# Cross-attention in fp32: a quarter of the score weights by a fast block algorithm, with three engines' work put in a new order

## The chip, the cores and the metric

The kernel runs on one NeuronCore of a Trainium2 chip. The core has a matrix engine (TensorE, PE in the profile; its weight loads are PEld), a vector engine (VectorE, DVE), an activation engine (ScalarE, ACT), a general engine (GpSimd, POOL) and a queue for transfers (SyncE, SP). The metric is device time in microseconds (us) of one execution. Everything is fp32.

## What is computed

```python
Q, K, V = x @ Wq, c @ Wk, c @ Wv        # 16 batches: x 256x256, c 77x192; 8 heads of 256
score = Q K^T / sqrt(256)                # per batch and head 256x77, masked
attn  = softmax(score)
out   = concat_heads(attn V) @ Wo + x
y     = (out - mean(out)) * rsqrt(var(out) + 1e-5) * gamma + beta
```

## The kernel before, in words

The kernel never forms Q, K or V. At the start it forms per head G = Wk Wq^T/16 (192 x 256; rows 0 to 127 in `gA`, the last 64 rows of two heads side by side in `gB`) and U = Wv Wo (in `uA`, `uB`). The context lies transposed, rows 0 to 127 in `cA` and the other 64 in both halves of `cB`. Then, for a group of GB = 4 batches and for each head, A = G^T c (256 x 308, as two halves `dc` of 128 rows), and scores are x A. For a batch, VW = c U.

A tile is 128 rows of x; a batch b has two tiles, 2b and 2b+1. The order of work is written out by hand: the program runs each engine's instructions as the code names them, and a wait on another engine blocks everything behind it on its own engine. The loop over batches `for b in range(-1, B - 1)` does in one step: scores of batch b+1 on TensorE (`scores`, L303), masking and row maximum on VectorE (`shift`, L320), exponentials on ScalarE (`exponential`, L340), weights on GpSimd (`weigh`, L361: exponentials times 1/sum into `p`), their transposition on VectorE (`turn`, L371), the sums of blocks that the next product needs on GpSimd (`sums`, L431 to L434; `differences`, L414), and for batch b the product of weights and VW by seven block products (`seven`, L450), whose results VectorE adds to x from PSUM (`add_product`, L498) and GpSimd from a copy `m` (`add_seven`, L484). For batch b-1 it takes the statistics of the rows (`finish`, L506 and L509 on VectorE), the inverse deviation (`spread`, L527 and L528 on ScalarE) and the normalisation (`normalise`, L548 and L577 on VectorE).

Every second step also prepares two batches ahead: `prepare_vw` (pv, L227 and L238) twice, and twice a pair of heads of A for the next group: `prepare_a` (pa), in part A with 128 rows of contraction (L193, four tiles of 128x32 of the array at a time) and in part B with 64 rows (L205, eight tiles of 64x32). ScalarE copies both out of PSUM (L963). PSUM is one pool of eight banks; a bank comes free when its last reader is through, and the next tile of the program takes the bank that has been free longest.

Of the kernel before, what the change touches and what calls it, by code (L numbers as in the profile page):

```python
# [27 lines left out]
def kernel(  # L28
# [53 lines left out]

    def by_dc(ap):
        return ap.rearrange("p (dc i c) -> p i dc c", dc=2, c=BK)
# [15 lines left out]
    cRA = const.tile([P, B, KR], F32, tag="cRA", name="cRA")  # L100
    cRB = const.tile([P, B, KR], F32, tag="cRB", name="cRB")
# [12 lines left out]

    def flat(ap):
        return ap.rearrange("p a b -> p (a b)")
# [51 lines left out]
    def prepare_a(g, places, lo=0, hi=GB, rest_first=False):  # L168
# [16 lines left out]
        def cols(dc, i):  # L185
            return slice((2 * i + dc) * BK, (2 * i + dc + 1) * BK)
# [29 lines left out]
        return part_A, part_B, copies  # L216

# [94 lines left out]
    def shift(t):  # L312


        b, ps = t // QT, ps_of.pop(t)
        s = sp.tile([P, H, S2], F32, tag="s", name=f"s_{t}")
        top = st.tile([P, H], F32, tag="top", name=f"top_{t}")
        for h in range(H):
            a, k = divmod(h, H // 2)
            nc.vector.tensor_tensor_reduce(  # L320
                s[:, h],
                ps[a][:, k * S2 : (k + 1) * S2],
                bias[:, b, :],
                scale=-1.0,
                scalar=FAR,
                op0=ALU.add,
                op1=ALU.min,
                accum_out=top[:, h : h + 1],
            )
        s_of[t] = s, top  # L330

# [105 lines left out]
    def seven(b):  # L437
# [36 lines left out]
        m = vwp.tile([P, 4, P], F32, tag="m", name=f"m_{b}", bufs=1)  # L474
# [3 lines left out]
    def add_seven(b):  # L478

        m = m_of.pop(b)  # L480
        y = x_of(QT * b, QT).rearrange("p t (c d) -> p t c d", c=2)

        def add(to, what):
            nc.gpsimd.tensor_tensor(to, to, what, ALU.add)  # L484

        for i in range(QT):
            add_product(QT * b + i)
# [12 lines left out]
    def finish(t):  # L500
        if t in po_of:
            add_product(t)
        g, j = t // GT, t % GT
        y = x_of(t)[:, 0, :]
        bn = st.tile([P, 6], F32, tag="bn", name=f"bn_{t}")
        nc.vector.bn_stats(bn, y)  # L506
        if j == 0:
            mv_of[g] = st.tile([P, GT, 2], F32, tag="mv", name=f"mv_{g}", bufs=2)
        nc.vector.bn_aggr(mv_of[g][:, j, :], bn)  # L509
# [12 lines left out]
    def spread(first, last):  # L522
# [4 lines left out]
        nc.scalar.activation(log[:, lo:hi], mv_of[g][:, lo:hi, 1], AF.Ln, bias=eps)  # L527
# [72 lines left out]
    with tc.tile_pool(name="wonce", bufs=1) as wp:  # L600
# [204 lines left out]
        def g_of(e):  # L805
# [6 lines left out]
            nc.scalar.mul(gA[:, e], pg, D ** -0.5)  # L812
# [15 lines left out]
        def g_of_pair(a):  # L828
# [12 lines left out]
            for e, o in enumerate(banks):  # L841
                nc.scalar.mul(gA[:, 2 * a + e], o, D ** -0.5)
# [42 lines left out]
        for a in range(1, NF):  # L885
# [7 lines left out]
            a_of_pairs(a, rest_first=True)  # L893
        load_x(0)
# [10 lines left out]
        for j in range(NF // 2):  # L905
# [13 lines left out]
            for e, pw in enumerate(  # L919
# [3 lines left out]
                for i in range(2):  # L923
                    for k in range(2):
                        copy(
                            of_e(uB, e)[half(k), :, 2 * j + i],
                            pw[half(i)].rearrange("p (n c) -> p n c", c=BK),
                        )
        for t in range(QT):
# [4 lines left out]
        turn_rest_last()  # L934
        sum_of(uB)
        for t in range(QT):
            exponential(t)
            weigh(t)

# [10 lines left out]
    def work_of(b, rest_first=False):  # L950
        g, n = b // GB + 1, b % GB
        work = [prepare_vw(b, rest_first)]
        if g < NG - 1 or g == NG - 1 and n < NF // 2:
            work.append(prepare_a(g, (n,), rest_first=rest_first))
        elif b <= NS:
# [11 lines left out]
    def turn_x_and_normalise(g, n, old):  # L967
        to_turn = (g, 0) if g < NG and n == 2 else (g - 1, GT // 2) if g > 1 and n == 0 else None
        if to_turn:
            for j in range(to_turn[1], to_turn[1] + GT // 2, 2):  # L970
                transpose_x(to_turn[0] * GT + j)
        if old:
# [4 lines left out]
    for b in range(-1, B - 1):  # L977
# [3 lines left out]
        for t in new if b >= 0 else ():  # L981
            scores(t)
        for t in new if b >= 0 else ():
            shift(t)
            if b == B - 2:
                finish(t - 2 * QT)
# [5 lines left out]
        for m in range(0, 2) if b < 0 else range(b + 2, min(b + 3, B // 2)):  # L992
            turn_last(m)
        alone = b + 1 >= B - GB // 2
        works = work_of(b + 1) if alone or n % 2 == 0 else []
        for part_A, _, _ in works:
# [21 lines left out]
        for i, t in enumerate(new if b >= 0 else ()):  # L1018
            exponential(t)
            if old:  # L1020
                finish(old[i])
            weigh(t)
        ahead = works and not alone
        if old and not ahead:
            spread(old[0], old[-1] + 1)
        if ahead:
            copy_out(works)
            if old:
                spread(old[0], old[-1] + 1)
# [3 lines left out]
            for part_A, _, _ in works:  # L1033
# [6 lines left out]
        if b < NS:  # L1040
            if now:
                seven(b)
            if old:
                invert(old[0], old[-1] + 1)
                normalise(old[0])
            for t in new:
                turn(t)
            if b < 0:
                for t in range(QT, GT, 2):
                    transpose_x(t)  # L1050
                bias_of(GB, B)
# [8 lines left out]
            if now:  # L1060
                add_seven(b)
# [56 lines left out]
```

## Time and profile before

| what | us |
|---|---|
| time before, median of 3 runs (270.31 to 270.97) | 270.63 |
| the profiled execution's own time | 269.95 |
| its span in the profile | 268.2 |
| busy: TensorE, VectorE, GpSimd, ScalarE | 262.5, 185.9, 173.2, 157.6 |

The profile has one row per group of instructions: line, engine, operation, what it writes and reads, shapes, count, total and mean time, and the idle time of the engine ahead of it with what ended that. The chain of waits follows the execution back from its last instruction and lists in order of time what each stretch of the span went to. Each fp32 matmul of the program is two instructions in the trace: sixteen matmuls of `prepare_a` stand there as x32.

### The profile page before, as it was taken

What the parts mean: (1) busy time and instruction counts of PE and PEld (TensorE: products, weight loads), DVE (VectorE), ACT (ScalarE), POOL (GpSimd) and SP (SyncE); (2) the same over time, 40 slices, a digit from 0 to 9 for tenths busy, and PEclk for the clock granted to TensorE, in tenths of its full rate; (3) what the DMA queues carried; (4) which work ended last, traced back from release to release, by engine and by line L of the source; (5) the groups of instructions that cost most, each with busy time, mean ns of one, the idle gap of its engine ahead of it and who ended that gap; (6) DMA issues with size and microseconds to landing.
All of it is one profiled execution on the core that took longest, in us unless ns stands there. A gap on an engine that the chain in (4) does not pass through costs nothing.

```text
span 268.2 us, 14455 instructions
## 1 busy us (share of the span) xinstructions
PE 262.5 (98%) x6090; PEld 191.8 (72%) x6090; DVE 185.9 (69%) x808; ACT 157.6 (59%) x667; POOL 173.2 (65%) x240
## 2 busy tenths in 40 slices
PE   8999999999999999999999999999999999999992
PEld 8566578944984699459944995499669957985662
DVE  1555967493583868665886379647977887799785
ACT  3243336536857565955596468737775595636772
POOL 1042005728399739994799669965998799585452
PEclk9999999999999999999999999999999999999999
DMA  6989987901500130232012401340034010100112
GB/s 190 217 199 228 334 138 142 311 21 34 129 7 2 46 80 2 63 111 71 5 43 90 112 5 43 91 113 2 6 120 122 4 45 2 44 22 22 46 40 80
DMA packets 41696, 22.69 MB, mean 85 GB/s; under 512 B 24144, under 2 KB 40608, under 8 KB 41632
## 3 DMA queue, kind: packets, MB, share of 16 engines
q1 hardware_dynamic: 41248, 20.98, 30.1%
q0 software_dynamic: 384, 0.79, 1.3%
q8 instruction: 48, 0.79, 1.3%
q14 instruction: 16, 0.13, 0.2%
HBM read 17.57 MB, written 4.19 MB: 81 GB/s over the span
## 4 chain that ended last, share of the span: by engine, by line
PE 98%; DVE 1%; issue 0%; DVEq 0%
PE ps L303 25%; PE pa L193 13%; PE pv L227 11%; PE po L450 11%; PE pm L450 8%; PE pa L205 6%; PE pv L238 6%; PE po L383 4%; PE pu L773 3%; PE pr L263 2%; PE pgb L834 2%; PE pw L787 1%; PE idle L703 1%; PE pr L274 1%; PE phb L850 1%; PE po L399 1%
## 5 line engine op out<-in xcount | busy, mean ns | idle before, releaser
L340 ACT ACTIVATE s<-s,top 128x77 f32<-128x77 f32 x256 | 85.3, 346 | 44.2 <-DVE top L320 37.9
L303 PE MATMUL ps<-a,xT 128*32 128x154 f32 x2048 | 69.9, 294 | 0.0
L303 PEld LDWEIGHTS ps<-a,xT 128*32 128x32 f32 x2048 | 66.2, 110 | 1.2 <-issue 0.4
L361 POOL TENSOR_TENSOR p<-s,rden 128x512 f32<-128x512 f32 x64 | 47.5, 768 | 29.5 <-DVE rden L355 29.4
L320 DVE CUSTOM_DVE_ANT_0 s<-ps,bias 128x77 f32<-128x77 f32 x256 | 43.5, 232 | 14.3 <-PE ps L303 14.3
L340 ACT ACTIVATION_READ_ACCUMULATOR s<-s,top 128x1 f32 x224 | 42.0, 187 | 0.0
L193 PE MATMUL pa<-cA,gA 128*32 128x308 f32 (+1 forms) x576 | 36.6, 395 | 0.0
L193 PEld LDWEIGHTS pa<-cA,gA 128*32 128x32 f32 x576 | 18.3, 110 | 21.0 <-issue 7.0
L484 POOL TENSOR_TENSOR xg<-xg,m 128x256 f32<-128x256 f32 x39 | 28.7, 736 | 6.6 <-DVE xg L498 4.5
L577 DVE SCALAR_TENSOR_TENSOR xg<-xg,rstd,bet 128x256 f32<-128x256 f32 x27 | 22.9, 847 | 14.0 <-ACT rstd L528 12.6
L227 PE MATMUL pv<-uA,cA 128*32 128x512 f32 x256 | 30.6, 595 | 0.0
L371 DVE STREAM_TRANSPOSE pT<-p 128x640 f32<-128x640 f32 x32 | 25.5, 821 | 3.4 <-POOL p L361 3.3
L414 POOL TENSOR_TENSOR ts<-vw 128x768 f32<-128x768 f32 x13 | 24.0, 1848 | 5.9 <-ACT vw L963 5.9
L963 ACT COPY vw<-pv 128x512 f32<-128x512 f32 x32 | 17.8, 584 | 14.8 <-PE pv L227 8.3
L498 DVE TENSOR_TENSOR xg<-po,xg 128x256 f32<-128x256 f32 x31 | 11.5, 405 | 13.8 <-PE po L450 13.3
L320 DVE DVE_READ_ACCUMULATOR2_ANT top<- 128x1 f32 x256 | 20.8, 81 | 0.0
L205 PE MATMUL pa<-cB,gB 64*32 64x308 f32 (+2 forms) x512 | 20.4, 387 | 0.0
L963 ACT COPY a<-pa 128x308 f32<-128x308 f32 (+1 forms) x56 | 18.9, 395 | 1.9 <-PE pa L193 0.4
L205 PEld LDWEIGHTS pa<-cB,gB 64*32 64x32 f32 (+1 forms) x512 | 11.0, 110 | 11.4 <-issue 6.2
L548 DVE SCALAR_TENSOR_TENSOR xg<-xg,mv,gam 128x256 f32<-128x256 f32 x30 | 17.6, 588 | 0.1
L238 PE MATMUL pv<-uB,cB 64*32 64x512 f32 x256 | 17.3, 597 | 0.0
L227 PEld LDWEIGHTS pv<-uA,cA 128*32 128x32 f32 x256 | 7.5, 109 | 12.8 <-issue 9.9
(119 smaller groups left out, 404.1 us busy)
## 6 DMA issues: line engine op xcount, KB each, us to landing
xg<-in_x_dram SPq DMA_DIRECT2D x8, 512.0 KB, 4.4
xT<-in_x_dram SPq DMA_DIRECT2D x56, 64.0 KB, 2.6
out_dram<-xg SPq DMA_DIRECT2D x11, 256.0 KB, 2.2
wo<-in_L_xattn_Wo_dram SPq DMA_DIRECT2D x4, 512.0 KB, 7.8
wq_blk<-in_L_xattn_Wq_dram SPq DMA_DIRECT2D x12, 128.0 KB, 4.3
out_dram<-xg SPq DMA_DIRECT2D x10, 128.0 KB, 1.9
wk_blk<-in_L_xattn_Wk_dram SPq DMA_DIRECT2D x12, 96.0 KB, 3.6
wvT<-in_L_xattn_Wv_dram POOLq DMA_DIRECT2D x8, 96.0 KB, 6.6
```

The costliest lines, as they stand in the source:

```text
L193: nc.tensor.matmul(flat(o[i * BK : (i + 1) * BK]), gA[:, h, cols(dc, i)], flat(cA[:, batches, :]), start=not rest_first and n in opening, ...
L205: nc.tensor.matmul(flat(banks[j + k][i * BK : (i + wide) * BK]), gB[half(k), h // 2, dc * P + i * BK : dc * P + (i + wide) * BK], flat(cB[ ...
L227: nc.tensor.matmul(pv[k][i * BK : (i + 1) * BK], cA[:, b, k * BK : (k + 1) * BK], uA[:, parts, :, i], start=not rest_first, stop=rest_first,)
L238: nc.tensor.matmul(pv[k][i * BK : (i + 1) * BK], cB[half(k), b, k * BK : (k + 1) * BK], uB[half(k), parts, :, i], start=rest_first, stop=n ...
L303: nc.tensor.matmul(ps[m // 2][i * BK : (i + 1) * BK, m % 2 * 2 * S2 : (m % 2 + 1) * 2 * S2], xT_of[t // PT][:, j * NM + m, dc], flat(a_of[ ...
L320: nc.vector.tensor_tensor_reduce(s[:, h], ps[a][:, k * S2 : (k + 1) * S2], bias[:, b, :], scale=-1.0, scalar=FAR, op0=ALU.add, op1=ALU.min ...
L340: nc.scalar.activation(s[:, h], s[:, h], AF.Exp, bias=top[:, one], scale=-1.0, accum_out=den[:, one] if summed_by_act(t) else None,)
L361: nc.gpsimd.tensor_tensor(part, e_mh[:, :, :, keys], rden_mh.unsqueeze(3).to_broadcast(list(part.shape)), ALU.mult,)
L371: nc.vector.transpose(pT_of[t].rearrange("p n m q -> p m n q"), p.rearrange("p m (n k) -> p m n k", k=BK),)
L450: nc.tensor.matmul(out[i * BK : (i + 1) * BK], weight[:, i], moving, start=first and n == 0, stop=final and n == len(terms) - 1,)
L484: nc.gpsimd.tensor_tensor(to, to, what, ALU.add)
L963: nc.scalar.copy(dst, src)
```

## The change

For 10 of the 12 pairs of heads in groups 1 to 3, A is computed by `prepare_fast` instead of `prepare_a`. With the 4 batches split into two of 154 columns and the 256 rows of A into two blocks of 128, the upper 128 rows of the contraction are a product of 2x2 blocks, done in seven block products; the 64 rows in `gB` take four more: 11 where 12 stood. Each has 64 rows of contraction and 128 rows of result, and runs as two 64x64 tiles of the array with 154 columns; two heads are walked together, one in each half of the rows. One block product per head is copied out of PSUM by ScalarE, and four additions per head on VectorE (`put_together`) make A out of the rest. The sums of blocks of G (`gS`, `gC`) are formed once, and those of c (`cT`, `cD`) at the start and once for each of groups 2 and 3, all on GpSimd with copies on ScalarE.

The loop up to batch 9 is rewritten as pairs of steps, `long_step` and `short_step`. In the long step all part As of `prepare_vw` come first, then `seven`, then part Bs, then the two fast pairs of heads. On GpSimd the weights of new tiles stand ahead of the additions of the previous batches (`add_blocks`), on VectorE the additions to x stand between the two turns, and the statistics of the first 14 tiles are taken by two ScalarE instructions each. From batch 9 on the loop is as before.

```diff
+    def sums_of_g():
+        for parts, sums, e, own, other in parts_of_g():
+            nc.scalar.copy(sums[own, 0, e], parts[other, 1, e])
+            nc.scalar.copy(gC[own], gB[other, :, P:])
+        for parts, sums, e, own, other in parts_of_g():
+            s1, s2, s3 = (sums[own, n, e] for n in range(3))
+            add(s1, s1, parts[own, 1, e])
+            subtract(s2, s1, parts[own, 0, e])
+            subtract(s3, parts[own, 0, e], parts[own, 1, e])
...
+    def sums_of_c(lo, hi):
+        xs, ys = halves_of(cA, lo, hi)
+        t1, t2, t3, t4 = (cT[:, n, lo - 1 : hi - 1] for n in range(4))
+        subtract(t1, ys, xs)
+        for own, other in ((low, high), (high, low)):
+            nc.gpsimd.tensor_copy(t2[own], ys[other])
+        subtract(t3, t2, ys)
+        subtract(t2, t2, t1)
+        for own, other in ((low, high), (high, low)):
+            nc.gpsimd.tensor_copy(t4[own], t2[other])
+        subtract(t4, xs, t4)
...
+    def prepare_fast(g, u):
...
+                for i in range(2):
+                    for ((bank, n), weight, moving), (start, stop, _) in zip(pair, flags):
+                        nc.tensor.matmul(
+                            bank[half(i), n],
+                            weight(i),
+                            moving,
+                            start=start,
+                            stop=stop,
+                        )
+                for ((bank, n), _, _), (_, _, one) in zip(pair, flags):
+                    if one:
+                        nc.scalar.copy(blocks[lone[id(bank)]][:, 0], by_batch(bank)[:, n])
...
+        def put_together(e):
+            mid, end, of = by_batch(mids[e]), by_batch(ends[e]), blocks[e]
+            plus(of[:, 3], mid[:, 2], of[:, 0])
+            plus(of[:, 1:3], mid[:, 0:2], of[:, 3:4].to_broadcast([P, 2, HB, S2]))
+            plus(of[:, 3], mid[:, 0], of[:, 2])
+            plus(of[:, 0:3], end, of[:, 0:3])
...
+        if by_act(t):
+            mean, var = (mv_of[g][:, j, n : n + 1] for n in range(2))
+            nc.scalar.activation(junk, y, AF.Identity, scale=1.0 / DI, accum_out=mean)
+            nc.scalar.activation(junk, y, AF.Square, bias=mean, scale=-1.0, accum_out=var)
+            return
...
         def turn_rest():
             nc.vector.transpose(flat(cA)[:, rest], flat(cA)[:, rest])
-            nc.gpsimd.tensor_copy(cRA, cA[:, :, KM:])
+            nc.scalar.copy(cRA, cA[:, :, KM:])
...
+    def long_step(b):
+        now, new, old = tiles_of(b), tiles_of(b + 1), tiles_of(b - 2)
+        g, n = (b + 1) // GB + 1, (b + 1) % GB
+        statistics(old)
+        if now:
+            scores_and_masks(new)
+            for t in new:
+                exponential(t)
+        while behind:
+            behind.pop(0)()
...
+        works = work_of(b + 1) + work_of(b + 2)
+        for part_A, *_ in works:
+            part_A()
+        if now:
+            seven(b)
+        for _, part_B, _ in works:
+            part_B()
+        fasts = []
+        for k in range(2):
+            fasts.append(prepare_fast(g, n + k))
+            if k == 0:
+                copy_out(works[:1])
+            fasts[k][0]()
+            if k == 0:
+                copy_out(works[1:])
...
+            for i, t in enumerate(new):
+                weigh(t)
+                for t in old[i : i + 1]:
+                    normalise(t)
+            add_blocks(b - 1)
+            turn(new[0])
+            add_products(b)
+            turn(new[1])
+            sums(b + 1)
+            add_blocks(b)
+            for k in range(2):
+                differences(b + 1 + k)
+            if n == 2 and g < NG - 1:
+                sums_of_c(g + 1, g + 2)
+        statistics(tiles_of(b - 1))
+        turn_some_x(g, n)
...
+        fasts[0][1](0)
+        fasts[0][1](1)
+        fasts[1][1](0)
+        behind.append(partial(fasts[1][1], 1))
```

The three pieces below show the order at the places that the steps of the sum speak of. TensorE, the preparation for batches 4 and 5, which lies between the scores of tiles 8 and 9 and those of tiles 10 and 11 (pv is VW, pa is A, pf is A by the fast way). Before, its head:

```order
L227 MATMUL pv_4_0_1850<-uA_79,cA_81 32x512 x4
L227 MATMUL pv_4_1_1851<-uA_79,cA_81 32x512 x4
L193 MATMUL pa_2_0_0_0_1853<-cA_81,gA_77 32x308 x4
L193 MATMUL pa_2_1_0_0_1854<-cA_81,gA_77 32x308 x4
L193 MATMUL pa_2_0_1_0_1855<-cA_81,gA_77 32x308 x4
L193 MATMUL pa_2_1_1_0_1856<-cA_81,gA_77 32x308 x4
L238 MATMUL pv_4_0_1850<-uB_80,cB_82 32x512
```

After, from the last products of `seven` for batch 3 (po) over the end of part B into the first fast pair of heads:

```order
L622 MATMUL po_3_1980<-ts_3_1594,pT_7_1916 32x128 x8
L404 MATMUL pv_4_0_1958<-uB_83,cB_85 32x512
...
L404 MATMUL pv_5_1_1962<-uB_83,cB_85 32x512
L361 MATMUL pf_2_0_0_2065<-cA_84,gA_77 64x154
L361 MATMUL pf_2_0_0_2064<-cA_84,gA_77 64x154
...
L361 MATMUL pf_2_0_0_2065<-cA_84,gS_518 64x154
L361 MATMUL pf_2_1_1_2067<-cA_84,gA_77 64x154
...
L361 MATMUL pf_2_1_1_2066<-cA_84,gA_77 64x154
```

The 308-column products in strips of 32 are gone, the 64x64 products of 154 columns stand at the end, and `seven` moved in between parts A and B.

VectorE, in the same stretch. Before, around the turns of tiles 8 and 9 (p is GpSimd's weights, po the product that is added to x):

```order
L509 BN_AGGR mv_0_1346<-bn_5_1930 128x2
L355 RECIPROCAL rden_9_1933<-den_9_1921 128x8
L548 SCALAR_TENSOR_TENSOR xg_1_518<-xg_1_518,mv_0_1346,gam_69 128x256
L577 SCALAR_TENSOR_TENSOR xg_1_518<-xg_1_518,rstd_4_1944,bet_90 128x256
L371 STREAM_TRANSPOSE pT_8_2086<-p_0_85 128x4x5x32
L371 STREAM_TRANSPOSE pT_9_2088<-p_1_86 128x4x5x32
L165 STREAM_TRANSPOSE xT_3_1441<-xT_3_1441 128x512 x2
...
L498 TENSOR_TENSOR xg_1_518<-po_3_2017,xg_1_518 128x256 x2
```

After, around the same turns in the long step:

```order
L527 RECIPROCAL rden_9_2174<-den_9_1944 128x8
L731 SCALAR_TENSOR_TENSOR xg_0_529<-xg_0_529,mv_0_1604,gam_69 128x256
L760 SCALAR_TENSOR_TENSOR xg_0_529<-xg_0_529,rstd_2_1835,bet_92 128x256
L543 STREAM_TRANSPOSE pT_8_2186<-p_0_87 128x4x5x32
L676 TENSOR_TENSOR xg_1_531<-po_3_1980,xg_1_531 128x256 x2
L543 STREAM_TRANSPOSE pT_9_2190<-p_1_88 128x4x5x32
L175 STREAM_TRANSPOSE xT_3_1617<-xT_3_1617 128x512 x2
L373 TENSOR_TENSOR a_2_2063<-pf_2_0_0_2064,a_2_2063 128x2x77
L373 TENSOR_TENSOR a_2_2063<-pf_2_0_0_2064,a_2_2063 128x4x77
```

The additions to x moved between the two turns, and the additions that make A stand behind them.

GpSimd at the start of the program, from its last loads to the sums of U (`uA`); nan and bias are the mask. Before:

```order
L618 DMA wvT_3_146<-in_L0_xattn_Wv_dram 32x6x128 x2
L594 TENSOR_TENSOR nan_0_621<-nan_0_621 128x4
L595 TENSOR_TENSOR nan_0_621<-nan_0_621 128x4
L596 TENSOR_TENSOR bias_89<-bias_89,nan_0_621 128x308
L902 TENSOR_TENSOR uA_79<-uA_79 128x512
L903 TENSOR_TENSOR uA_79<-uA_79 128x512
```

After:

```order
L801 DMA wvT_3_148<-in_L0_xattn_Wv_dram 32x6x128 x2
L245 TENSOR_TENSOR gS_518<-gS_518,gA_77 64x4x128
L246 TENSOR_TENSOR gS_518<-gS_518,gA_77 64x4x128
L247 TENSOR_TENSOR gS_518<-gA_77 64x4x128
...
L777 TENSOR_TENSOR nan_0_634<-nan_0_634 128x4
L778 TENSOR_TENSOR nan_0_634<-nan_0_634 128x4
L779 TENSOR_TENSOR bias_91<-bias_91,nan_0_634 128x308
L1087 TENSOR_TENSOR uA_82<-uA_82 128x512
L1088 TENSOR_TENSOR uA_82<-uA_82 128x512
L255 TENSOR_TENSOR gS_518<-gA_77,gS_518 64x4x128 x2
```

Six operations on blocks of G now stand ahead of the mask, and two more behind the sums of U.

More of the change, by code (lines that the diff above doesn't have):

```diff
@@ L526, in spread @@
         rstd = st.tile([P, GT], F32, tag="rstd", name=f"rstd_{first}")
-        nc.scalar.activation(log[:, lo:hi], mv_of[g][:, lo:hi, 1], AF.Ln, bias=eps)
+        nc.scalar.activation(log[:, lo:hi], mv_of[g][:, lo:hi, 1], AF.Ln, bias=eps, scale=1.0 / DI if by_act(first) else 1.0)
         nc.scalar.activation(rstd[:, lo:hi], log[:, lo:hi], AF.Exp, scale=-0.5)
@@ L976, with tiles_of, statistics, scores_and_masks @@
     last = NT - 1
-    for b in range(-1, B - 1):
+    def tiles_of(b):
+        return range(b * QT, (b + 1) * QT) if b >= 0 else ()
+    def statistics(tiles):
+        for t in tiles:
+            finish(t)
+        if tiles:
+            spread(tiles[0], tiles[-1] + 1)
+            invert(tiles[0], tiles[-1] + 1)
+    between = []
+    def scores_and_masks(new, to_finish=()):
+        for t in new:
+            scores(t)
+        for i, t in enumerate(new):
+            shift(t)
+            for t in to_finish[i : i + 1]:
+                finish(t)
+            while between:
+                between.pop(0)()
@@ new lines, in short_step, with last_turn @@
+    def short_step(b):
+        new = tiles_of(b + 1)
+        scores_and_masks(new)
+        for t in new:
+            exponential(t)
+        seven(b)
+        weigh(new[0])
+        for _ in range(2):
+            if behind:
+                behind.pop(0)()
+        for m in range(b + 2, min(b + 3, B // 2)):
+            turn_last(m)
+        weigh(new[1])
+        turn(new[0])
+        def last_turn():
+            turn(new[1])
+            sums(b + 1)
+            add_products(b)
+            if b + 1 == ready:
+                add_blocks(b)
+        between.append(last_turn)
@@ L978 @@
+    ready = B - GB - GB // 2 - 1
+    for b in range(-1, ready, 2):
+        long_step(b)
+        short_step(b + 1)
+    statistics(tiles_of(ready - 2))
+    behind.extend(partial(normalise, t) for t in tiles_of(ready - 2))
+    for b in range(ready, B - 1):
         old = range(max(b - 1, 0) * QT, b * QT)
@@ L980 @@
         new = range((b + 1) * QT, (b + 2) * QT)
[L981 to L986, printed above, removed]
+        scores_and_masks(new, old if b == B - 2 else ())
         while behind:
@@ L991 @@
             load_x((g * GB + n) // 2)
-        for m in range(0, 2) if b < 0 else range(b + 2, min(b + 3, B // 2)):
-            turn_last(m)
         alone = b + 1 >= B - GB // 2
-        works = work_of(b + 1) if alone or n % 2 == 0 else []
-        for part_A, _, _ in works:
+        ahead = not alone and n % 2 == 0
+        works = work_of(b + 1) if alone or ahead else []
+        for part_A, *_ in works:
             part_A()
@@ L1040 @@
         if b < NS:
[L1041 to L1045, printed above, removed]
+            seven(b)
+            invert(old[0], old[-1] + 1)
+            normalise(old[0])
             for t in new:
                 turn(t)
[L1048 to L1051, printed above, removed]
             if alone or ahead:
```

176 lines of the change are left out of this document (149 added, 27 removed).

## The prediction

> **What bounds the kernel now.** I read the page's busy line and its chain first, then the chain in order of time, then the groups.
>
> ```profile
> PE 262.5 (98%) x6090; PEld 191.8 (72%) x6090; DVE 185.9 (69%) x808; ACT 157.6 (59%) x667; POOL 173.2 (65%) x240
> PE 98%; DVE 1%; issue 0%; DVEq 0%
> ```
>
> TensorE is busy for 98% of the span, and 98% of the chain lies on it. The chain in time order (start, length) shows that it never pauses:
>
> ```profile
> 17.16 2.21 PE pa L193 x32
> 19.37 1.03 PE phb L850 x32
> 20.41 1.73 PE pgb L834 x32
> ...
> 130.76 4.19 PE ps L303 x128
> 134.95 1.72 PE pv L227 x16
> 136.67 2.07 PE pa L193 x32
> 138.74 1.02 PE pv L238 x16
> 139.76 1.04 PE pa L205 x32
> 140.79 0.86 PE pv L238 x16
> 141.65 1.04 PE pa L205 x32
> 142.69 1.85 PE pv L227 x16
> 144.54 2.07 PE pa L193 x32
> 146.62 1.75 PE pm L450 x64
> 148.37 2.17 PE po L450 x64
> 150.54 4.19 PE ps L303 x128
> ...
> 263.37 0.30 DVE xg L516
> ```
>
> Each stretch starts where the last one ended; the tail off TensorE begins at 263.37. So the change gains only what it takes from TensorE's own work, and loses whatever wait it opens there.
>
> **TensorE's own work.** Two pairs of heads of A take 2 × (2.07 + 1.04) = 6.22 us in each pair of steps (136.67 and 139.76, 141.65 and 144.54). They become 2 × 44 matmuls of 64x64 tiles with 154 columns, 88 trace instructions for each pair of heads. No row shows this shape. The nearest by columns is ps: 4.19/128 = 32.7 ns each at 154 columns, four tiles at a time. The nearest by tile are pgb and phb (64x64): 1.73/32 = 54 ns at 256 columns, 1.03/32 = 32.2 ns at 128. At 256 columns a 64x64 tile costs 0.211 ns a column, ps 0.212: the same pace. At 128 it costs more than that pace (27 ns), because loading weights fills the time:
>
> ```profile
> 19.37:20.41 1.04, 1.04 (x37) 1.01 (x40) 0.00 (x0) 0.42 (x1) 1.04 (x3) 1.00 0.88 208
> ```
>
> (TensorE busy 1.04, weight loads busy 1.01 of 1.04 us.) At 154 columns the columns themselves need 32.6 ns by that pace, as much as the loads took there, so I take ps's 32.7: 88 × 32.7 = 2.88 us. As upper bound, the straight line between phb and pgb gives 32.2 + 26/128 × 21.8 = 36.6 ns, 3.22 us; phb's 1.03 also holds the change of tile shape behind pa, so this is generous. Lower bound: 154 × 0.211 = 32.5 ns, 2.86 us.
>
> Changing the shape of the tiles costs something: pv in part A takes 1.72 behind ps (both 128x32) but 1.85 behind part B, and part B 1.02 against 0.86. Before, each pair of steps has two such changes. After, there are three: part A and `seven` (both 128x32) to part B (64x32), part B to the fast products (64x64), these to the scores (128x32). The middle one keeps 64 rows and changes only the columns; no row shows that alone. I take 0.13, the smaller of the two seen; bounds 0 and 0.16.
>
> Here a rule bears. The Trainium skill (TensorEngine Tiling (Array Packing), Key Properties) says that changing the tiling mode, unlike moving to another tile of the same mode, drains TensorE. By that rule the middle change costs like the others (gain 1.7 us in all), without it nothing (2.3 us); the rows 1.85 and 1.02 agree with a drain where the number of rows changes, and no run here shows the other kind.
>
> Sum for a pair of steps: 6.22 − 2 × 2.88 − 0.13 = 0.33 us; five pairs: 1.65 us. Bounds: 6.22 − 5.72 = 0.50 (2.5 in all), and 6.22 − 6.44 − 0.16 = −0.38 (1.9 slower in all). `seven` and pv keep their shapes, so their move costs TensorE nothing.
>
> **The other engines' work** in a pair of steps, from the busy row of one (VectorE, ScalarE, GpSimd: third to fifth) and the groups:
>
> ```profile
> 130.76:158.64 27.88, 27.88 (x713) 20.22 (x708) 18.59 (x96) 18.15 (x82) 22.53 (x30) 1.00 0.21 60
> L498 DVE TENSOR_TENSOR xg<-po,xg 128x256 f32<-128x256 f32 x31 | 11.5, 405 | 13.8 <-PE po L450 13.3 <-PE po L383 0.5
> L516 DVE TENSOR_TENSOR xg<-po,xg 128x128 f32<-128x128 f32 x2 | 0.6, 286 | 0.0
> L506 DVE BATCH_NORM_STATS2 bn<-xg 128x6 f32<-128x256 f32 x31 | 12.3, 396 | 0.1
> L509 DVE BATCH_NORM_AGGREGATE mv<-bn 128x2 f32<-128x6 f32 x31 | 5.6, 182 | 1.1
> L963 ACT COPY a<-pa 128x308 f32<-128x308 f32 x40 | 15.3, 437 | 1.5
> L963 ACT COPY a<-pa 128x154 f32<-128x154 f32 x16 | 3.5, 292 | 0.4 <-PE pa L193 0.4
> L561 ACT ACTIVATE xg<-xg,rstd 128x256 f32<-128x256 f32 x3 | 1.5, 510 | 0.3 <-DVE xg L548 0.2
> L340 ACT ACTIVATION_READ_ACCUMULATOR s<-s,top 128x1 f32 x224 | 42.0, 187 | 0.0
> L903 POOL TENSOR_TENSOR uA<-uA 128x512 f32<-128x512 f32 x1 | 1.3, 1275 | 0.1
> L484 POOL TENSOR_TENSOR m<-m 128x128 f32<-128x128 f32 x26 | 11.9, 457 | 3.1 <-ACT m L475 2.1
> ```
>
> - VectorE: by the two additions (286 ns at 128 elements, 405 at 256; 0.93 ns an element) a head's four additions of 154, 308, 154 and 462 cost 0.31 + 0.45 + 0.31 + 0.60 = 1.67 us, four heads 6.7. Statistics of four tiles leave: 4 × 0.578 = 2.3. 18.6 + 6.7 − 2.3 = 23.0 of 27.6.
> - ScalarE: eight copies of 308 leave (3.5), four of 154 come (1.2), and eight statistics passes (510 + 187 ns each, 5.6): 18.2 − 3.5 + 1.2 + 5.6 = 21.5.
> - GpSimd: 22.5, and in two pairs of steps the sums of c: four of 154 (0.55 each by L484) and four copies (under that), at most 4.4: 26.9.
>
> All fit under 27.6, so none becomes the bound by its load; the question is lateness. Moved loads of x land two pairs of steps ahead of their use and are priced at nothing; what hides them is that distance.
>
> **Where TensorE could wait.** Time runs from the start of a long step's scores (0). Scores end at 4.19, part A at 7.6, `seven` at 11.55, part B at 13.4; the fast products run from 13.6 to 19.3. The first pair of heads needs four banks: two that `shift` frees (by 4.9), one freed by ScalarE's copy m, and one, at its third block products (14.1), freed by the second addition to x, which now stands on VectorE behind the turn of the first new tile.
>
> ```profile
> 124.11 0.36 ACT L340 ACTIVATE s<-s,top 128x77 f32<-128x77 f32 x1 [2.92 <-DVE top L320]
> ...
> 129.60 0.28 ACT L527 ACTIVATE log<-mv,eps 128x2 f32<-128x2 f32 x1
> 128.95 3.16 POOL L361 TENSOR_TENSOR p<-s,rden 128x512 f32<-128x512 f32 x4 [3.36 <-DVE rden L355]
> ```
>
> Two tiles' exponentials take 5.5 us there (124.11 to 129.60). With ScalarE's statistics ahead of them (2.8 us and 0.5 for the deviation, begun when the short step's copy m is out) they run from about 3.6 to 9.1; VectorE then normalises (1.4), turns the first tile by 11.4 and adds to x by 12.4, after `seven` at 11.55. Margin 1.7 us. GpSimd's weights for a tile (1.6) are ready before. The next scores, at 19.3, need the first head's banks: the first pair of heads ends at 16.4, its first head is put together by 18.1, the second by 19.8 (needed 21.4). Margins 1.2 and 1.6. The mask of the next tile starts some 0.8 us late, which ScalarE's idle 2.92 covers. I price waits at nothing; what is late next if this fails is the mids bank at 14.1.
>
> **The start of the program.** GpSimd gets six sums of G (1.28 each by L903: 7.7 us) ahead of the mask:
>
> ```profile
> 40.16 0.20 POOL L594 TENSOR_TENSOR nan<-nan 128x4 f32<-128x4 f32 x1 [18.46 <-DVE nan L593]
> 40.72 0.70 POOL L596 TENSOR_TENSOR bias<-bias,nan 128x308 f32<-128x308 f32 x1
> 44.91 0.24 DVE L320 CUSTOM_DVE_ANT_0 s<-ps,bias 128x77 f32<-128x77 f32 x1
> ```
>
> It idled 18.46 us there. The sums start when ScalarE has copied A's last banks and the first block, near 32.5, and end near 40.2: just in front of the mask. The mask is ready at 41.4 and wanted at 44.91, so 3.5 us are left.
>
> **Sum.** The profiled execution took 269.95, 0.68 below the median: 269.95 − 1.65 = 268.3 on its scale, 270.63 − 1.65 = 269.0 on the median's.
>
> **Rivals.**
> 1. *Short columns cost more.* The straight line's 36.6 ns would make the pair 0.35 longer than before: 270.63 + 1.75 = 272.4; halfway (34.7 ns) it saves nothing: 270.6. For it: phb. Against it: its loads, not its columns, set that time, and ps shows nothing extra at 154. The Trainium skill (TensorEngine Tiling (Array Packing), Instruction Overhead) speaks for it, with about 60 cycles for each matmul. The trace's ps row does not bear it out: 154 columns at 32.7 ns are half of pa's 64.7 at 308. Chance 0.14.
> 2. *Lateness on VectorE and ScalarE eats the gain.* If the additions for A run 40% slower beside GpSimd (2.35 us a head), three heads end at 23.5 instead of 21.5, the next mask starts 2.0 us later than priced, ScalarE with it, and the margin of 1.7 at 14.1 is gone: TensorE waits 0.3 us a pair, which cancels the gain. For it: VectorE's load grows most, and GpSimd is busy 22.5 of 27.9 beside it. Against it: the additions' rows above are means beside a busy GpSimd already. Time 270 to 271. Chance 0.15.
> 3. *Slower: the mask at the start.* If a sum on 64 partitions takes 2.5 us instead of 1.28, the six end 7.3 later, the mask is 3.8 late, and TensorE waits in `prepare_last` for the banks of tile 0's scores some 2.5 to 4 us: 272. It decides from about 2.1 us a sum. Against it: no row of this size on GpSimd is above 1.28. Chance 0.05.
> 4. Forecast as worked out: 268.1 to 269.9. Chance 0.66.
>
> **How the numbers follow.** 0.2% (0.54 us) is about what a measurement of this kernel can tell from none. Faster takes the forecast and a part of rivals 1 and 2: 0.71. Same: 0.16, from the middle of 1 and 2. Slower: 0.13, from the ends of 1 and 2 and from 3. The range reaches from the lower bound of the products (2.5 off: 268.1, and 0.1 for the runs' scatter) to where rival 2 ends: 268.0 to 271.0.
>
> **What would show it.** In the profile after: pf at 2.9 us for each pair of heads, `ps` right behind it, no idle time on TensorE before 262; VectorE near 23 busy in a pair of steps, ScalarE near 21. Wrong if pf takes over 3.1, or a stretch on the chain is VectorE, ScalarE or GpSimd before the tail.

## The result, and the profile after

| | before | after |
|---|---|---|
| time, median (range), us | 270.63 (270.31 to 270.97) | 268.83 (268.58 to 269.66) |
| the profiled execution, us | 269.95 | 268.58 |
| its span, us | 268.2 | 266.8 |

The ratio is 0.9939, with a 95% interval of 0.992 to 0.9958: faster by 0.6%, 1.8 us in the medians and 1.4 us between the two profiled executions. The forecast was 269.0 (268.0 to 271.0).

The busy line and the chain of the profile after:

```profile
PE 260.5 (98%) x6330; PEld 202.8 (76%) x6330; DVE 212.7 (80%) x860; ACT 166.9 (63%) x710; POOL 191.5 (72%) x272
PE 96%; DMA 2%; DVE 1%; SPq 0%; issue 0%; DVEq 0%
```

TensorE has 240 instructions more and 2.0 us less work, and it still carries the chain. The three engines beside it all got more. Next, one pair of steps from the chain in order of time (start, length, what), the two fast pairs of heads in it as `pf`:

```profile
94.18 4.32 PE ps L469 x128
...
100.25 2.17 PE po L622 x64
102.42 4.19 PE ps L469 x128
...
113.96 1.88 PE pv L404 x32
115.84 5.93 PE pf L361 x176
121.76 4.32 PE ps L469 x128
```

Each row begins where the last one ended (in the rows left out too), so TensorE waits for nobody here. The pair lasts from 94.18 to 121.76, 27.58 us; before it lasted 27.88. The 176 instructions of `pf` took 5.93 us, 33.7 ns each, 2.97 for each pair of heads. (Ten of the 16 pairs of heads, four in each of four groups of batches, are made this way; "a quarter" in the title is not their share.) The rows also show three changes of tile shape: `pv` L404 takes 1.88 behind `po` (1.72 is twice the 0.86 that half of it took before, behind products of its own shape), `ps` takes 4.32 behind `pf` and 4.19 behind `po`, and `pf` is 0.17 longer than 176 times `ps`'s 32.7 ns (5.76).

The busy rows of three pairs of steps (length; then TensorE, weight loads, VectorE, ScalarE, GpSimd, each with its instructions; granted clock, DMA) show the load beside TensorE:

```profile
94.18:121.76 27.58, 27.58 (x756) 22.64 (x760) 25.36 (x105) 20.57 (x95) 23.54 (x36) 1.00 0.22 61
121.76:149.35 27.59, 27.59 (x757) 22.66 (x760) 24.66 (x105) 20.57 (x95) 21.77 (x31) 1.00 0.23 61
149.35:176.94 27.59, 27.59 (x757) 22.65 (x760) 23.64 (x103) 20.70 (x95) 24.33 (x37) 1.00 0.21 57
```

VectorE is busy for 23.6 to 25.4 of 27.6 us, and TensorE has no gap. What makes this possible stands in two rows of the timeline of VectorE, in the long step whose scores start at 102.42:

```profile
113.70 0.83 DVE L543 STREAM_TRANSPOSE pT<-p 128x640 f32<-128x640 f32 x1
114.46 0.71 DVE L676 TENSOR_TENSOR xg<-po,xg 128x256 f32<-128x256 f32 x2
```

The additions to x (L676) end at 115.17. The bank that the second of them frees is wanted by the third block products, some 0.5 us behind the start of `pf`, at about 116.3. The margin is about 1.1 us.

The start of the first product of v in each pair of steps is a clock that leaves out the start of the program, which scatters by some tenths from run to run:

| kernel | from pair 1 to pair 6, us | the five pairs |
|---|---|---|
| before | 135.51 | 23.98, 27.88, 27.89, 27.88, 27.88 |
| after | 134.04 | 23.69, 27.58, 27.59, 27.59, 27.59 |

(The first is shorter, since the first step has less work.) All five are 0.29 to 0.30 shorter, 1.47 us in all; the two profiled executions differ by 1.37, and the tenth between them lies at the start. The medians differ by 1.80, so by 0.33 more than the five pairs. The profiles do not show where that comes from: the one profiled execution before was 0.68 under its median, and the first scores come anywhere from 41.8 to 42.8 us in the profiles of this document.

### The profile page after: what moved, and what is told of

Same layout as the page of the kernel before. It is cut to its first block, busy times and chain, and to the rows that moved or that the text cites. A ratio compares the mean times of both kernels' runs of the same rounds, so it can differ in the third digit from the quotient of the medians.

```text
span 266.8 us, 15067 instructions
## 1 busy us (share of the span) xinstructions
PE 260.5 (98%) x6330; PEld 202.8 (76%) x6330; DVE 212.7 (80%) x860; ACT 166.9 (63%) x710; POOL 191.5 (72%) x272
## 3 DMA queue, kind: packets, MB, share of 16 engines
HBM read 17.57 MB, written 4.19 MB: 82 GB/s over the span
## 4 chain that ended last, share of the span: by engine, by line
PE 96%; DMA 2%; DVE 1%; SPq 0%; issue 0%; DVEq 0%
PE ps L469 25%; PE pf L361 11%; PE po L622 11%; PE pv L393 10%; PE pm L622 9%; PE pv L404 6%; PE pa L203 5%; PE po L555 4%; PE pu L956 3%; PE pa L215 2%; PE pr L429 2%; PE pgb L1017 2%; DMA wq_nat<-in_L_xattn_Wq_dram 2%; PE pw L970 1%; PE pr L440 1%; PE phb L1033 1%
## 5 line engine op out<-in xcount | busy, mean ns | idle before, releaser
L486 DVE CUSTOM_DVE_ANT_0 s<-ps,bias 128x77 f32<-128x77 f32 x256 | 43.3, 232 | 4.6 <-PE ps L469 4.0
L373 DVE TENSOR_TENSOR a<-pf,a 128x154 f32<-128x154 f32 x80 | 33.9, 435 | 7.3 <-PE pf L361 4.9
L543 DVE STREAM_TRANSPOSE pT<-p 128x640 f32<-128x640 f32 x32 | 26.3, 827 | 5.1 <-POOL p L533 5.0
L393 PE MATMUL pv<-uA,cA 128*32 128x512 f32 x256 | 29.6, 593 | 0.0
L1150 ACT COPY vw<-pv 128x512 f32<-128x512 f32 x32 | 17.1, 587 | 14.9 <-PE pv L404 14.9
L760 DVE SCALAR_TENSOR_TENSOR xg<-xg,rstd,bet 128x256 f32<-128x256 f32 x27 | 22.7, 840 | 2.6 <-ACT rstd L711 1.2
L586 POOL TENSOR_TENSOR ts<-vw 128x768 f32<-128x768 f32 x13 | 23.6, 1831 | 0.0
L486 DVE DVE_READ_ACCUMULATOR2_ANT top<- 128x1 f32 x256 | 20.9, 82 | 0.0
L731 DVE SCALAR_TENSOR_TENSOR xg<-xg,mv,gam 128x256 f32<-128x256 f32 x30 | 18.0, 600 | 0.1
L361 PE MATMUL pf<-cT,gS 64*64 64x154 f32 x240 | 17.4, 290 | 0.0
L603 POOL TENSOR_TENSOR ss<-pT 128x256 f32<-128x256 f32 x13 | 9.7, 745 | 9.8 <-DVE pT L543 9.7
L404 PE MATMUL pv<-uB,cB 64*32 64x512 f32 x256 | 16.3, 596 | 0.0
L622 PE MATMUL po<-vr,pT 128*32 128x256 f32 x208 | 16.0, 379 | 0.0
L361 PEld LDWEIGHTS pf<-cT,gS 64*64 64x64 f32 x240 | 15.8, 133 | 0.0
L203 PE MATMUL pa<-cA,gA 128*32 128x308 f32 (+1 forms) x256 | 14.0, 360 | 0.0
```

Of the source, the lines that this page charges most:

```text
L203: nc.tensor.matmul(flat(o[i * BK : (i + 1) * BK]), gA[:, h, cols(dc, i)], flat(cA[:, batches, :]), start=not rest_first and n in opening, ...
L361: nc.tensor.matmul(bank[half(i), n], weight(i), moving, start=start, stop=stop,)
L373: nc.vector.tensor_tensor(out, *of, ALU.add)
L393: nc.tensor.matmul(pv[k][i * BK : (i + 1) * BK], cA[:, b, k * BK : (k + 1) * BK], uA[:, parts, :, i], start=not rest_first, stop=rest_first,)
L404: nc.tensor.matmul(pv[k][i * BK : (i + 1) * BK], cB[half(k), b, k * BK : (k + 1) * BK], uB[half(k), parts, :, i], start=rest_first, stop=n ...
L486: nc.vector.tensor_tensor_reduce(s[:, h], ps[a][:, k * S2 : (k + 1) * S2], bias[:, b, :], scale=-1.0, scalar=FAR, op0=ALU.add, op1=ALU.min ...
```

## Experiments

Two theories went in. One: TensorE's shorter products of A are the gain, and the order of the other engines' work is of little account, since their loads fit beside it. Two: the loads fit only in the new order; in the old one the products would open waits that eat the gain. Each kernel's text says what its theories expect of it.

**The changed kernel once more**, beside the experiments that undo a part of it:

> The changed kernel unaltered, as the measure for the three beside it. Expected 268.8 us again (268.6 to 269.2), a pair of steps at 27.59 us on TensorE.

268.91 us (268.64 to 269.11), ratio to before 0.9929 (0.9911 to 0.9947). This is what the next kernels are compared with.

**The new order with the old products.**

```diff
+        olds = [prepare_a(g, (n,))]
+        olds[0][0]()
...
-        fasts = []
-        for k in range(2):
-            fasts.append(prepare_fast(g, n + k))
...
+        olds[0][1]()
+        copy_out(works)
+        olds.append(prepare_a(g, (n + 1,), rest_first=True))
+        olds[1][1]()
+        olds[1][0]()
+        copy_out(olds)
...
```

> The new order of the work on the other engines stays (statistics of x on ScalarE, GpSimd's weights ahead of its block additions, VectorE's additions to x between the turns), but A is made as before: 128x154 and 128x308 products in two pieces for each pair of heads, copied by ScalarE, with no putting together on VectorE. Theory 1, the gain is TensorE's shorter products of A and nothing else: a pair of steps takes 27.8 to 27.9 us again and the time is 270.3 to 270.7. Theory 2, the new order alone already frees something that TensorE waited for before: 269.5 or less. Theory 3, the old products in the new order find ScalarE late (its copies of A come back beside the statistics it has been given) and TensorE waits: over 271.5.

270.4 us (269.91 to 270.56), ratio 0.9986 (0.9974 to 0.9999). The chain of a pair:

```profile
142.93 2.07 PE pa L203 x32
145.00 1.88 PE pv L404 x32
146.88 2.09 PE pa L215 x64
148.96 2.21 PE pa L203 x32
151.17 4.19 PE ps L469 x128
```

The old products take 2.07 + 2.09 + 2.21 = 6.37 us here, and the pairs take 27.89 to 27.90 us, as before. TensorE has no gap in them. So the order by itself brings nothing that these pairs show (theory 1 of that text), and the gain comes with the products.

**The statistics of x back on VectorE.**

```diff
-        return t // QT < B - 2 * GB - 1
+        return False
```

> All statistics back on VectorE; the rest as changed. Theory 1 (TensorE's own work decides and nobody waits): 268.8 us, within 0.2. In the changed kernel's trace VectorE adds to x 12.0 to 12.8 us after a long step's scores start, and the bank is wanted at 13.9; two tiles' statistics (1.16 us) ahead of the mask move ScalarE's exponentials by about 0.5 us only, since ScalarE loses its own 2.4 us there. Theory 2 (the new order on the other engines carries part of the gain): VectorE rises from 25 to 27 us of 27.6 in a pair of steps and TensorE waits 0.3 us or more in each of four pairs: 270.0 us or above.

272.12 us (271.94 to 273.02), ratio 1.0052 (1.0032 to 1.0072): 3.2 us over the changed kernel and slower than before, as theory 2 had it. VectorE's timeline in the same long step (its scores start at 103.04 here):

```profile
118.21 0.43 DVE L691 BATCH_NORM_STATS2 bn<-xg 128x6 f32<-128x256 f32 x1 [0.57 <-POOL xg L664]
118.67 0.18 DVE L692 BATCH_NORM_AGGREGATE mv<-bn 128x2 f32<-128x6 f32 x1
119.02 0.43 DVE L691 BATCH_NORM_STATS2 bn<-xg 128x6 f32<-128x256 f32 x1 [0.16 <-POOL xg L664]
...
120.89 5.42 DVE L373 TENSOR_TENSOR a<-pf,a 128x154 f32<-128x154 f32 x12
126.23 0.23 DVE L486 CUSTOM_DVE_ANT_0 s<-ps,bias 128x77 f32<-128x77 f32 x1
```

The statistics (0.6 us a tile) stand ahead of A's additions (L373) and wait there for GpSimd's additions to x (0.57 and 0.16 us). The next mask (L486) starts 23.2 us behind the long step's scores, where in the changed kernel it starts 21.2 behind them (123.61, from 102.42). Two steps later the chain runs over GpSimd, and the second to fifth pairs are 27.59, 27.72, 29.29 and 28.65: three of the four are late, not all as theory 2 expected. TensorE waits there for `seven`'s sums (L605), for A (L373) and for the addition to x (L676), 0.3 to 0.6 us at a time.

**GpSimd's block additions ahead of its weights**, as before the change:

```diff
+            add_blocks(b - 1)
             for i, t in enumerate(new):
                 weigh(t)
...
-            add_blocks(b - 1)
```

> GpSimd's additions of the previous batch ahead of the weights again in the long step. They take 3.35 us. Theory 1: the weights of the first new tile end near 12.1 instead of 9.0 after the scores start, VectorE turns and adds by 13.6, just ahead of 13.9: no more than 0.1 us in a pair, 268.8 to 269.3 us. Theory 2: the wait for the bank opens in every pair by 0.5 us or more: 270.8 us or above.

270.36 us (269.98 to 270.84), ratio 0.999 (0.9977 to 1.0003): 1.45 over the changed kernel, between the two forecasts and four fifths of the gain. The second to fifth pairs are 27.59, 27.89, 27.59 and 28.77, so two are late. The row of TensorE's waits (waiter, releaser: us in all, times, longest):

```profile
PE pf L361 <- DVE xg L676: 1.0, 1, 1.0
```

That is the place named in the prediction: the third block products wait for the addition to x. The chain into that wait, in the fifth pair:

```profile
171.24 0.84 DVE pT L543
172.09 0.65 DVE xg L676 x2
...
172.88 5.47 PE pf L361 x160
```

Two long steps earlier, in the pair of 27.89, VectorE's timeline shows the first turn itself waiting for the weights, with the addition behind it:

```profile
114.89 0.85 DVE L543 STREAM_TRANSPOSE pT<-p 128x640 f32<-128x640 f32 x1 [1.28 <-POOL p L533]
115.66 0.72 DVE L676 TENSOR_TENSOR xg<-po,xg 128x256 f32<-128x256 f32 x2
```

The additions end at 116.38, just when the block products want the bank, and that pair is 0.3 us longer.

**VectorE's additions to x behind both turns:**

```diff
             turn(new[0])
-            add_products(b)
             turn(new[1])
+            add_products(b)
```

> VectorE's additions to x behind both turns again in the long step. Theory 1: the second turn (0.75 us) goes first, so the additions end at 13.5 after the scores start, still ahead of 13.9: 268.8 us, within 0.2. Theory 2: the bank comes late in every pair, 0.4 us each in four pairs: 270.4 us.

269.32 us (268.94 to 269.66), ratio 0.9943 (0.9925 to 0.9962). The second to fifth pairs are 27.59, 27.58, 27.59 and 27.84: only the last one is longer, by a quarter of a microsecond. That is nearer to theory 1, and above its range. The rest of the 0.4 us is not accounted for: the first scores came at 42.76 us here, at 41.98 and 42.42 in the two profiles of the changed kernel, but the edit leaves the start as it was. The margin of 1.1 us covers one turn of 0.83.

**All three undone at once: the products without these three moves.** The rest of the new order, TensorE's own above all, stays.

> The new products of A with the old order on the other engines: statistics of x on VectorE, GpSimd's block additions ahead of its weights, VectorE's additions to x behind both turns. Theory 1, each of the three moves only takes a wait away that the others would have left, and the waits of the three experiments before lie one behind another on one chain, so they cover each other: about as slow as the costliest alone (statistics on VectorE, 3.2 us): 272 to 272.8. Theory 2, they are separate waits and add up (3.2 + 1.45 + 0.4): 273.5 to 275. Either way the new products without the new order are slower than the kernel before. Rival: below 270.6, the products bring something even alone.

277.78 us (276.06 to 278.01), ratio 1.0234 (1.0192 to 1.0277): 8.9 over the changed kernel, against 5.1 for the three added up. Neither forecast for it holds, and the rival (still faster) least of all. One wait makes most of it:

```profile
PE pf L361 <- DVE xg L676: 6.2, 4, 2.4
```

The chain that leads into the longest of the four:

```profile
113.67 0.80 POOL xg L664
114.47 0.07 issue
114.54 0.80 POOL xg L664
115.34 2.87 POOL p L533 x4
...
118.22 0.85 DVE pT L543
119.07 0.65 DVE xg L676 x2
...
119.86 3.39 PE pf L361 x95
```

Block additions, weights, the second turn, the additions to x, the block products: each waits for the one ahead. In the single experiments, as far as their rows show it, a link of this chain was missing. Where only the block additions had been put back, the additions to x stood behind the first turn and so needed the first tile's weights alone (TensorE waited 1.0 us, once). Where only the additions to x had been put back, both tiles' weights were ready early (0.25 us, once). With both put back the whole chain stands ahead of the block products. The two moves are two ways round one wait, and the price of undoing both can't be read from undoing each. What share the statistics on VectorE have in the 8.9 was not separated.

TensorE was also busy for 264.1 us against 260.5. A part of that is its clock, the last column but two of these busy rows:

```profile
119.86:123.25 3.39, 3.39 (x104) 3.39 (x108) 3.22 (x10) 1.56 (x4) 3.15 (x7) 1.00 0.38 130
...
180.95:186.24 5.29, 5.29 (x120) 5.08 (x118) 4.42 (x11) 0.98 (x4) 5.05 (x7) 0.72 0.01 3
```

Behind the wait of 2.37 us at 117.49 the granted clock stayed at 1.00. Behind that of 1.95 us which ended at 179.09 it was halved for 3.41 us, from 180.45 to 183.86, some 1.7 us lost; the 0.72 is the mean of a row that holds only a part of that stretch. The last section says what tells the two waits apart.

**How much less TensorE could do before another engine binds.** Two kernels leave block products out.

```diff
-            return list(zip(ones, m[:1] + o[:3] + m[1:] + o[3:]))
+            every = list(zip(ones, m[:1] + o[:3] + m[1:] + o[3:]))
+            return [pair for i, pair in enumerate(every) if i not in (6,)]
...
```

> Leaves one of the 11 block products of each head out (the seventh), so that one block of A lacks a term; everything else stays. Theory 1, TensorE alone sets the time: 16 instructions fewer in each pair of steps at 32.7 ns, 0.52 us, five times, so 2.6 us less than the changed kernel: about 266.2. Theory 2, the engines beside it are already at their limit with 11 products: 268 or more.

266.6 us (266.38 to 266.67), ratio 0.9849 (0.9829 to 0.9868). The pairs are 27.06 to 27.07, 0.52 to 0.53 shorter, as 16 instructions at 32.7 ns say. Of the 2.6 us in five pairs 2.3 reached the medians (2.1, if each kernel is taken against the one before beside it); 0.19 went right behind the fifth pair, where the next products of v came after 25.03 us for 24.84. With `if i not in (5, 6, 9)`:

> Leaves three of the 11 block products of each head out (the sixth, seventh and tenth), so that A lacks terms; everything else stays. Theory 1, TensorE alone sets the time: 48 instructions fewer in each pair of steps at 32.7 ns, 1.57 us, five times, so 7.8 us less than the changed kernel: about 261. Theory 2, VectorE (23.5 to 25.4 of 27.6 us busy in a pair of steps, with turns that can't be moved) or the margins of about 1 us for the second addition to x and below nothing for the mask hold the pair at 26.5 to 27.2 us: 263.5 to 267.

265.01 us (264.63 to 265.19), ratio 0.9794 (0.9771 to 0.9816): 3.9 us less, half of the 7.8 forecast. TensorE's waits show who holds it:

```profile
PE pm L626 <- POOL ts L590: 1.5, 2, 0.8
PE pm L626 <- POOL ss L609: 0.5, 1, 0.5
```

The pairs of steps are 22.39, 26.22, 27.52, 26.21 and 27.84. The first, second and fourth follow TensorE, which is busy without a gap; they are 1.30 and 1.38 shorter than in the changed kernel, not 1.57, since the 128 instructions of `pf` left take 35.5 ns each (4.55 us). The third and fifth are 1.3 and 1.6 longer than that, and in them `seven` waits for GpSimd's sums. So with 11 products the kernel has about one product per head left before the engines beside TensorE bind; with three fewer, they do in two pairs of five. That VectorE is one of them is argued, not shown by an experiment of its own: in these two pairs it is busy for 26.4 and 26.6 us, more than the 26.2 that TensorE needs, in the second and fourth for 19.6 and 21.8.

**The price of a change of tile shape.** Eight small products are put ahead of the first block products of each pair of heads, in columns of the bank that nothing reads:

```diff
...
+            for n in range(8):
+                rows, m = (low, 64) if n % 2 else (low, 32)
+                nc.tensor.matmul(
+                    spare[1][:m],
+                    gA[rows, heads[0], :m],
+                    flat(cA[rows, 0:1, :BK]),
+                    start=True,
+                    stop=True,
+                )
             for pair in pairs():
```

The control has `(low, 64)` for all, the third kernel `(slice(0, P), 64)` for every other one.

> The control for the price of a change of tile shape: eight small products more ahead of the first of each pair of heads' products (80 in all), each 64 rows by 64 columns of weights and 32 columns moved, into columns of the bank that nothing reads. All in the shape of the products that follow. Estimate from the row of the products themselves: a product that runs alone in one of four places, with a weight load beside it, 0.03 to 0.13 us each, so 2 to 10 us for 80.

> As the control, but every other one of the eight has 32 columns of weights instead of 64, which makes 14 more changes of shape in a pair of steps, 70 in all. Theory 1, a change of shape between 64x64 and 64x32 costs 0.13 to 0.17 us, as the first products of A behind v's paid: 9 to 12 us over the control. Theory 2, those 0.17 us are something else (the first weight load of a group, the first use of a bank) and a change is free: within 2 us of the control.

> As the control, but every other one of the eight has 128 rows of weights instead of 64, 15 more changes of shape in a pair of steps, 75 in all, now in the rows. Theory 1, a change costs the same 0.13 to 0.17 us whichever side changes: 10 to 13 us over the control. Theory 2, rows cost and columns do not, or the other way round: this one and the one with 32 columns differ by 5 us or more. Theory 3, neither costs: both within 2 us of the control.

They took 278.43, 284.62 and 287.26 us (one run each; before, beside them, 270.63). The small products (L354) in the chain of the control:

```profile
118.08 1.88 PE pv L415 x32
119.96 0.99 PE pf L354 x15
...
123.91 0.85 PE pf L354 x15
124.76 2.97 PE pf L372 x86
```

The second group of eight in the chain of the kernel with 64x32:

```profile
126.27 1.55 PE pf L354 x15
```

And in that with 128x64:

```profile
128.06 1.78 PE pf L354 x15
```

In the control the eight take 0.99 behind `pv` (64x32) and 0.85 behind block products (64x64): the one change of shape there costs 0.14, as in the changed kernel. In the second group, eight changes of the columns cost 1.55 − 0.85 = 0.70, 0.09 each, and eight of the rows 1.78 − 0.85 = 0.93, 0.12 each. Both cost, the rows somewhat more; these runs do not separate the change itself from what a small product of the other shape takes. The sizes forecast (9 to 12 and 10 to 13 us over the control) were too high: 6.2 and 8.8. A likely reason, not tested, is that the small products run one behind another anyway, 0.11 us each in the control, so that less is left to drain than behind products that fill all four tiles.

**The block products in narrower tiles**, which saves one change of shape in a pair:

```diff
-                for i in range(2):
+                for i in range(4):
...
-                            bank[half(i), n],
-                            weight(i),
+                            bank[i * BK : (i + 1) * BK, n],
+                            weight(i // 2)[:, i % 2 * BK : (i % 2 + 1) * BK],
```

> The block products of A run as four tiles of 64x32 in place of two of 64x64: twice the instructions, eight tiles at a time, the shape of the products of v that stand ahead of them, so one of the three changes of shape in a pair of steps goes. Theory 1, the columns set the pace (half of 32.7 ns a product): the same 5.76 us without the 0.17 behind v, five times: 0.7 to 0.9 us less, about 268.1. Theory 2, loading the weights or issuing sets a floor above 16.4 ns (16 loads of 64x32 took 0.18 us ahead of v's products, 11 ns each; the loads of the shape 64x64 fill all of the present 32.7): at 20 to 27 ns for each of 352 instructions the pair takes 1.2 to 3.6 us more, 275 to 287.

287.16 us (285.59 to 288.17), ratio 1.0613 (1.0586 to 1.0641). The time is at the upper end of theory 2's range, but not for its reason. The chain behind `pv`:

```profile
121.59 2.35 PE pf L361 x142
123.95 0.64 issue
124.59 2.33 PE pf L361 x127
126.92 1.45 issue
128.37 1.76 PE pf L361 x83
```

While they run, 142 products take 2.35 us, 16.5 ns each: the columns do set the pace, as theory 1 had it. But 142 products in, and again 127 products later, TensorE stands still, for nothing that the profile shows as a wait ("issue"). The row of its waits:

```profile
PE pf L361 <- issue: 11.1, 9, 2.4
```

These 11.1 us in 9 pauses are most of the loss of 18.3; the last section comes back to them.

No experiment gave a version that beats the changed kernel and computes all of A.

## Why the prediction was right, step by step

- **TensorE's pace at 154 columns**: taken as `ps`'s 32.7 ns, 2.88 us for a pair of heads. In TensorE's timeline of the changed kernel a round of four products starts every 131 ns (41 rounds from 116.08 to 121.47 us), 32.9 ns a product. Rival 1 (34.7 to 36.6 ns) is out: even with the change of shape counted in, it is 33.7.
- **The change of shape in the columns**: taken as 0.13, with 0 as a bound; measured 0.14 (the control) and 0.17 (`pf`). The length of a change fits what a drain costs: the first round ends a whole product's 290 ns behind the last one of the other shape, where rounds of one shape end 131 ns apart. The rule of the Trainium skill (TensorEngine Tiling (Array Packing), Key Properties), that a change of tiling mode drains TensorE, agrees with the rows where only the columns change: 0.14 behind full products, 0.09 each among small ones. It gives no price.
- **The sum**: 0.33 a pair was forecast, 0.29 to 0.30 measured; 1.65 in five pairs against 1.47. The 0.18 that lacks is the pace and the change of shape, a few hundredths of a pair each. The medians differ by 1.80, on the other side of the forecast, and 0.33 of that no profile shows. So that 268.83 came so near to 269.0 is in part luck.
- **Loads**: VectorE 23.0 forecast, 23.6 to 25.4 measured. The forecast started from 18.59, the least of four pairs of steps before (18.59 to 19.65). Its normalisation there is 4.7 us (L548 and L577), after it is 5.8 to 6.7 (L731 and L760), which the forecast took as unchanged; why they take longer no run shows. The additions for A are the smaller part. Their groups after:

```profile
L373 DVE TENSOR_TENSOR a<-pf,a 128x462 f32<-128x462 f32 x20 | 12.8, 640 | 1.0
L373 DVE TENSOR_TENSOR a<-pf,a 128x154 f32<-128x154 f32 x40 | 12.4, 310 | 5.6 <-PE pf L361 4.9
L373 DVE TENSOR_TENSOR a<-pf,a 128x308 f32<-128x308 f32 x20 | 9.6, 479 | 0.7
```

  640 + 2 × 310 + 479 ns is 1.74 us a head for 1.67, 0.3 a pair of steps. ScalarE took 20.6 for 21.5, GpSimd 21.8 to 24.3 for 22.5 to 26.9.
- **Waits priced at nothing**: right, there is none between 6 and 262 us. The margins were smaller than worked out. The bank of the third block products had 1.1 us for 1.7: the additions ended at 12.75 for 12.4, behind two normalisations whose L760 took 1.16 us each (L577 took 0.85 in the mean before), and the bank was wanted at 13.9 for 14.1. The next mask was 0.6 late for 0.8: it started 1.9 us behind its scores (123.61, from 121.69), where one that waits for TensorE alone starts 1.3 behind (131.12, from 129.82). "What is late next" was named rightly: the three experiments in which TensorE waits at `pf` all wait there, for L676.
- **The start**: the six sums of G ended at 40.6 (1.26 to 1.29 us each, forecast 40.2) and the mask at 42.6 (forecast 41.4), wanted at 45.05. Rival 3 is out, with 2.4 us left for 3.5: the mask waited for VectorE's reduction (L776), which the prediction did not follow.
- **Where it was luck**: rival 2 had 0.15, at 40% slower additions. In the kernel without the statistics on ScalarE VectorE is late by as much as that rival has it, for another reason: the next mask starts 2.0 us later (23.2 for 21.2). It costs 3.2 us, where rival 2 was priced at 0.3 a pair. The price was too low: it counted one pair's lateness, and the pairs of 27.72, 29.29 and 28.65 us show that the later ones lose more. With 1.1 us in hand where 1.7 had been worked out, that no wait opened was in part luck.

## What to carry to other kernels

A gain on the bounding engine is worth its full amount only while the other engines keep their order, and that order has no value of its own: here the products without three moves of it cost 7 us, the order alone brought 0.1, and both together saved 1.8. Undo moves together as well as one by one, since two moves can guard the same wait. And when TensorE's work is cut into more tile shapes, count the changes of shape: at 0.14 to 0.17 us each behind full products, one change took a third of the 0.46 that a pair would have gained without it.

## What was not expected of the hardware

- **Instructions can run out.** In the narrow-tile kernel TensorE ran 127 products and as many weight loads in 2.33 us and then paused; 254 instructions lie between two pauses, and the nine pauses are 0.5 to 2.4 us long. The row of the transfer queue that carries instructions in that kernel (packets, MB, share of time):

```profile
q8 instruction: 57, 0.93, 1.4%
```

  That is 16.3 KB a packet. The changed kernel has 50 of them: seven fewer, with 880 products and 880 weight loads fewer, 251 instructions a packet. The Trainium skill (Runtime: NRT & Kernel Launch, Instruction fetch mechanics) says that instructions are refilled in blocks of 16 KiB, 256 of them, and that the cost of a boundary is mostly hidden. The trace agrees on the size and shows when it is not hidden: a block used up in 2.33 us. Its list of transfers shows why: each of the nine pauses ends 1.2 to 1.5 us behind the end of such a packet (the packet that ended at 126.99 and the pause that ended at 128.37, 157.12 and 158.57), and two packets never start less than 3.35 us apart, in this kernel as in the changed one. With 64x64 tiles the same number of instructions takes 4.2 us (128 × 32.7 ns) and no pause shows. That the pauses are refills is inferred from these times; no kernel with a pace between the two was run.
- **What decides when the granted clock falls.** In the same kernel it was 0.70 in the mean of a row behind a pause of 2.40 us:

```profile
156.17:158.57 2.40, 0.00 (x0) 0.00 (x0) 1.91 (x5) 2.24 (x9) 2.24 (x5) 1.00 0.02 7
158.57:161.79 3.22, 3.22 (x126) 2.74 (x126) 1.32 (x4) 0.53 (x3) 3.14 (x4) 0.70 0.02 5
```

  The 0.70 is again a mean: the clock was 0.50 from 159.83 to 163.24, for 3.41 us, and 1.00 around it. The Trainium skill (TensorE: Matmul & The Clock Gate, Part 1) gives an idle window of about 3.4 us that runs on its own. The trace agrees on the length and that it runs on its own: in both profiles the changes lie whole multiples of 3.41 us apart (159.83, 163.24 and, at the end, 282.71 here; 180.45, 183.86 and 276.02 in the kernel without the three moves). But a window need not be idle throughout. Counted in these windows, the half clock followed where TensorE was busy for 1.26 us (156.42 to 159.83 here) or 1.46 (177.04 to 180.45 there) of the 3.41. It did not follow where it was busy for 1.75 (146.31 to 149.72 there) or 1.79 (187.13 to 190.54 here), and the wait of 2.37 us lay across two windows, busy for 1.89 and 2.54. So what counts, as far as these two traces go, is how much of one window is idle, with the limit somewhere between 1.66 and 1.95 us, and not how long a wait is. That is read from these stretches alone; no experiment was made of it.
